# Reordering the booked steps of a Mamba layer's side work around its scans

## The chip, the cores and the metric

The kernel runs on one core of a Trainium2 chip. The metric is the device time of one execution in microseconds (us). A core has five engines that run side by side, each taking its own instructions in program order: TensorE (PE, matrix products into PSUM), VectorE (DVE), ScalarE (ACT, functions and copies), GpSimd (POOL) and SyncE (SP, here the queue that starts most of the DMAs). They wait for each other by semaphores.

## What is computed

The reference is a stack of four pre-normalised residual layers on `x` of shape (2, 128, 56, 56): agent attention, a 3x3 convolution, a mixture of patch experts, and a pair of Mamba scans over image rows. Only the last is touched here. For one way (forward, "f"; "b" runs the row backwards) it is:

```
xi, z = split(x @ in_w.T)
xc = silu(conv_b + sum_k pad(xi)[k : k + L] * conv_w[:, k])
dt, B, C = split(xc @ xproj_w.T, [8, 24])
dt = softplus(dt @ dt_w.T + dt_b)
h[l] = exp(dt[l] * A) * h[l-1] + (dt[l] * xc[l]) * B[l]      # 16 states a channel
y = (sum_s h[l, s] * C[l, s] + xc * D) * silu(z)
out = y @ out_w.T
```

The two ways' results are joined by `fuse_w`, normalised over the channels (mean and variance, scale `ln_w`, shift `ln_b`) and added to `x`.

## The kernel before

`mamba_pair` (from L1532) cuts the work into 14 blocks of 448 positions (8 rows of 56). Each block has two `Half` objects, f and b, and each half has 16 units: 8 pairs of states times two halves of the 256 channels. A unit is one step of the main loop, so a block is a period of `STEPS` = 32 steps: 0 to 15 for f, 16 to 31 for b.

Step n issues, in this order:

- ACT: `decay(n+1)`, two exponentials (L1822) into a `dA` tile in PSUM. There are two such tiles, so it waits until scan n-1 has read its own.
- The fetches due at this step: ACT operations that empty a PSUM bank which PE filled in an earlier step.
- In even steps, unless POOL makes this pair's product: `read_out`, an ACT copy of the pair's C row into the PSUM tile `c_ps` (L1840). In even steps also `send_c`, the DMAs of a later pair's C rows (SP, L1751).
- POOL: `push(n+3)`, the product `dBu` (L1833), four buffers.
- DVE: `scan(n)` (L1852). In odd steps the product of the pair's states with C follows: on DVE from `c_ps` (L1861), or on POOL (L1858) for the pairs in `POOLED`, which are 0, 3, 6 of f and 0, 3 of b. These are steps 0-1, 6-7, 12-13, 16-17 and 22-23.
- DVE: `close`, the gating of y (L1878), when a half's products are all collected. PE: `collect` of the unit three steps back (L1872).
- `run(n)`: the stages booked for this step by hand.

The order of the last item is what the change edits. `book(step, stage, tag, late)` puts a stage in a list; `run` calls it at its step, and if the stage returns a function, that function is the fetch of step + 1 + late. The tag names the PSUM bank that the stage's product takes: "mm" or "c", one bank each, and "c" is also `c_ps`'s bank. A stage that takes a bank waits, on PE, until its last reader is done.

While period p scans block p, the booked stages prepare block p+1, end the preparation of block p's b half and finish block p-1. For a half they are `conv(0)`, `conv(1)` (PE L1703, fetched on ACT L1712 into `xc`), `silu` (L1883 to L1886: a table load, silu of this half's `xc`, silu of the same way's gates `zs` of the block before, and a table load back), `low` (PE L1732, fetched on ACT L1735 into `low`), `send_low` (SP: L1740, L1745), `step(m)` (PE L1757; its fetch is four ACT operations L1767 to L1771), `error(m)` (DVE L1777), `log(m)` (ACT L1782, reads the bank of `step`), `softplus(m)` (PE L1787, fetched by ACT L1788), `weigh` (POOL L1795, L1799), `send_steps` (SP L1810) and `gate(m)` (PE L1720, fetched by ACT L1727). `sp_e` and `sp_u` have one buffer each; `weigh` writes its product over `sp_u`, and the DMAs of `send_steps` read it from there. The finishing of a block is `fuse` (PE L1624, fetched by ACT L1635), `measure` (DVE L1641), `root` (ACT L1648), `newton` (DVE L1657), `normalize` (four ACT operations, L1665), `turn_back` (PE L1676, fetched by ACT L1680) and `onto` (POOL L1686, output DMA L1688).

Of the kernel before, what the change touches and what calls it, by code (L numbers as in the profile page):

```python
# [1531 lines left out]
def mamba_pair(net, out, wts, combine):  # L1532
# [19 lines left out]
    with ExitStack() as ctx:  # L1552
# [327 lines left out]
        def silu(inputs, gates):  # L1880

            if inputs:
                nc.scalar.activation(inputs.xc, inputs.xc, AF.Silu)  # L1883
            if gates:
                nc.scalar.activation(gates.zs, gates.zs, AF.Silu)
            nc.scalar.preload_act_table_set(EXP_LN)  # L1886

        blocks = [Block(b, k) for b in range(NB) for k in range(NBLK)]
# [3 lines left out]
        def book(step, *stages, tag="mm", late=0):  # L1892

            agenda.setdefault(step, []).extend((stage, tag, late) for stage in stages)

        for n, blk in enumerate(blocks):

            f, b = blk.ways
            at = STEPS * (n - 1)
            if n == 0:  # L1900

                book(at + 1, blk.norm)
                book(at + 3, lambda f=f: f.conv(0))
                book(at + 4, lambda f=f: f.conv(1), tag="c")
                book(at + 6, lambda f=f: silu(f, None))
                book(at + 7, f.low)
                book(at + 9, lambda f=f: f.step(0))
                book(at + 9, lambda f=f: f.step(1), tag="c", late=1)
                book(at + 9, f.send_low)
                for m in range(2):  # L1910
                    book(at + 10 + m, lambda f=f, m=m: f.error(m))
                    book(at + 10 + m, lambda f=f, m=m: f.log(m))
                    book(at + 11 + m, lambda f=f, m=m: f.softplus(m), tag=("mm", "c")[m])
                    book(at + 12 + m, lambda f=f, m=m: f.weigh(m))
                    book(at + 12 + m, lambda f=f, m=m: f.send_steps(m))
                for i, (h, m) in enumerate(((f, 0), (f, 1), (b, 0), (b, 1))):
                    book((1, 4, 5, 13)[i], lambda h=h, m=m: h.gate(m))
                book(at + 17, lambda b=b: b.conv(0))
                book(at + 17, lambda b=b: b.conv(1), tag="c")
                book(at + 19, lambda b=b: silu(b, None))  # L1920
                for m in range(2):
                    book(2 + 3 * m, lambda b=b, m=m: b.step(m))
                    book(3 + 3 * m, lambda b=b, m=m: b.error(m))
                    book(4 + 3 * m, lambda b=b, m=m: b.log(m))
                    book(7 + m, lambda b=b, m=m: b.softplus(m))
                book(0, b.low)
                book(2, b.send_low)
                book(11, b.weigh, b.send_steps)
            else:
                before = blocks[n - 1]  # L1930
                book(at + 6, blk.norm)
                book(at + 7, lambda f=f: f.conv(0))
                book(at + 8, lambda f=f: f.conv(1), late=1)
                book(at + 10, lambda f=f, g=before.ways[0]: silu(f, g))
                book(at + 12, lambda b=b: b.conv(0))
                book(at + 12, lambda b=b: b.conv(1), tag="c", late=1)
                book(at + 15, f.low, tag="c")
                book(at + 17, f.send_low)
                book(at + 17, lambda f=f: f.step(0))
                book(at + 18, lambda b=b, g=before.ways[1]: silu(b, g))  # L1940
                book(at + 19, lambda f=f: f.error(0))
                book(at + 19, lambda f=f: f.log(0))
                book(at + 20, lambda f=f: f.step(1))
                book(at + 21, lambda f=f: f.error(1))
                book(at + 22, lambda f=f: f.log(1))
                book(at + 22, lambda f=f: f.softplus(0), tag="c")
                book(at + 23, b.low)
                book(at + 24, lambda f=f: f.softplus(1))
                book(at + 25, f.weigh)
                book(at + 26, lambda f=f: f.gate(0))  # L1950
                book(at + 27, lambda b=b: b.step(0))
                book(at + 27, f.send_steps)
                book(at + 28, lambda b=b: b.error(0))
                book(at + 28, lambda b=b: b.log(0))
                book(at + 29, lambda b=b: b.step(1))
                book(at + 31, lambda b=b: b.error(1))
                book(at + 31, lambda b=b: b.log(1))
                book(at + 32, lambda b=b: b.softplus(0), tag="c")
                book(at + 33, lambda f=f: f.gate(1), late=1)
                book(at + 33, lambda b=b: b.softplus(1), tag="c")  # L1960
                book(at + 33, b.send_low)
                book(at + 35, lambda b=b: b.gate(0))
                book(at + 38, b.weigh)
                book(at + 43, b.send_steps)
                book(at + 46, lambda b=b: b.gate(1), late=1)

            at = STEPS * (n + 1)
            book(at + 4, lambda blk=blk: blk.fuse(0))
            book(at + 4, lambda blk=blk: blk.fuse(1), late=1)
            book(at + 6, blk.measure)  # L1970
            book(at + 7, blk.root, tag="c", late=1)
            book(at + 7, blk.newton)
            book(at + 15, blk.normalize)
            book(at + 16, blk.turn_back)
            book(at + 31, blk.onto)
        for h, step in zip(blocks[-1].ways, (10, 18)):
            book(STEPS * (len(blocks) - 1) + step, lambda h=h: silu(None, h))

        units = [(h, u) for blk in blocks for h in blk.ways for u in range(UNITS)]
# [71 lines left out]
def layers(tc, a, out, wide, attention):  # L2051
    with ExitStack() as ctx:
        net = Net(ctx, tc, a)
        keep = ctx.enter_context(tc.tile_pool(name="keep2", bufs=1, side="right"))
        with tc.tile_pool(name="l1_keep", bufs=1) as taps:
# [5 lines left out]
            with tc.tile_pool(name="l2_w", bufs=2) as wpool:  # L2061
# [44 lines left out]
                with tc.tile_pool(name="l2_work", bufs=2, reuse_waits="tile") as work, tc.tile_pool(  # L2106
                    name="l2_ps", bufs=2, space=PSUM
                ) as ps:
                    experts.run(wpool, work, ps)
        mamba_pair(net, out, wts, experts.combine)  # L2110


# [34 lines left out]
```

## Time and profile before

| What | us |
| --- | --- |
| Median of three runs | 3112.28 |
| The three runs | 3108.09, 3112.28, 3123.26 |
| The profiled execution | 3107.69 |
| Its span | 3105.9 |
| Scan of the first unit starts at | 1731.7 |
| Busy over the span: PE, DVE, ACT, POOL | 2688.7, 2225.7, 1825.4, 1491.6 |
| L1833, POOL, 448 times | 2130 ns each |
| L1852, DVE, 448 times | 2007 ns each |
| L1861, DVE, 154 times | 2021 ns each |
| L1858, POOL, 70 times | 3989 ns each |
| L1822, ACT, 896 times | 636 ns each |

The Mamba layer is the part from 1731.7 us on, somewhat under half of the span. In what follows, a line of the timeline gives the start in us, the length in us, engine, line, operation, what it writes and reads with shapes, how many instructions were merged into it, and in brackets how long the engine had been idle before it and what released it. DVE and ACT instructions that follow each other overlap by about a tenth of a microsecond, so starts are better guides than ends.

### The profile page before, as it was taken

The page shows a single profiled execution, that of the slowest core. Times are in us where ns is not written, and L with a number is a line of the kernel's source. Part 1 is how long each engine was busy: PE and PEld are TensorE (multiplying, and loading weights), DVE is VectorE, ACT ScalarE, POOL GpSimd, SP SyncE. Part 2 cuts the span into 40 slices and gives each one's busy share as a digit, 9 for nine tenths or more (in the row PEclk, how much of TensorE's full clock was granted, in tenths as well). Part 3 has the DMA queues.
Part 4 walks back from the last instruction along what each step waited for, and adds up shares of the span by engine and source line. Part 5 has one row for each costly group of instructions (what it writes and reads, how often), then busy time and mean ns, then how long its engine had stood idle before and what let it go on. Part 6 is the DMA issues. An engine that isn't in the chain of part 4 may idle for free. (4 is left out here: it accounts for less than half of the span.)

```text
span 3105.9 us, 34183 instructions
## 1 busy us (share of the span) xinstructions
PE 2688.7 (87%) x12348; PEld 1055.9 (34%) x12348; DVE 2225.7 (72%) x2033; ACT 1825.4 (59%) x2788; POOL 1491.6 (48%) x801
## 2 busy tenths in 40 slices
PE   7999999999998899999996877888778887778774
PEld 3333333332334444444443322323223333223221
DVE  5879999999887111111112699999999999999996
ACT  5778788887641011111111678777787877777774
POOL 3000100100521000000003799999999999999995
PEclk9999999999998899999997888988888888889886
DMA  1000000000011878787773654564555545545550
GB/s 54 1 1 1 1 1 1 1 1 1 1 38 42 324 280 320 285 318 293 308 299 105 141 115 111 111 142 111 113 126 112 128 112 126 126 109 115 129 125 23
DMA packets 157914, 368.98 MB, mean 119 GB/s; under 512 B 25156, under 2 KB 114980, under 8 KB 154132
## 3 DMA queue, kind: packets, MB, share of 16 engines
q1 hardware_dynamic: 135744, 339.30, 38.0%
q0 software_dynamic: 5520, 15.62, 1.6%
q10 hardware_dynamic: 16452, 11.61, 1.2%
q8 instruction: 101, 1.65, 0.2%
q14 instruction: 97, 0.79, 0.1%
HBM read 297.89 MB, written 17.20 MB: 101 GB/s over the span
## 5 line engine op out<-in xcount | busy, mean ns | idle before, releaser
L1833 POOL TENSOR_TENSOR dBu<-dtu,Bs 128x896 f32<-128x896 f32 x448 | 937.3, 2130 | 61.5 <-DVE h L1852 51.6
L1852 DVE TENSOR_TENSOR_SCAN h<-dA,dBu 128x896 f32<-128x896 f32 x448 | 880.0, 2007 | 64.6 <-ACT dA L1822 47.7
L620 ACT ACTIVATE ex<-sc 128x896 f32<-128x896 f32 (+1 forms) x700 | 602.6, 917 | 124.4 <-PE sc L617 113.2
L1872 PE MATMUL y<-h,both 128*64 128x448 f32 x1792 | 484.1, 639 | 66.4 <-POOL h L1858 55.4
L627 DVE TENSOR_TENSOR ex_sum<-ex_sum,ex 128x1792 f32<-128x1792 f32 (+1 forms) x238 | 492.6, 2070 | 35.1 <-ACT ex L620 21.1
L617 PE MATMUL sc<-q,k 32*128 32x448 f32 (+1 forms) x2800 | 403.4, 587 | 3.6 <-ACT ex L620 2.9
L1341 PE MATMUL h_ps<-w,xs_c 128*128 128x512 f32 x896 | 393.1, 597 | 10.3 <-issue 10.3
L635 PE MATMUL av<-ex,va 128*32 128x448 f32 (+1 forms) x2800 | 334.3, 552 | 0.1
L1861 DVE TENSOR_TENSOR h<-h,c_ps 128x1792 f32<-128x1792 f32 x154 | 311.3, 2021 | 25.5 <-ACT c_ps L1840 10.6
L1822 ACT ACTIVATE dA<-dt,f_A 128x448 f32<-128x448 f32 x448 | 283.8, 636 | 72.9 <-DVE h L1852 48.2
L582 POOL TENSOR_TENSOR a_e<-a_e,a_inv 112x784 f32<-112x784 f32 x14 | 41.6, 2974 | 582.8 <-ACT ex L620 394.5
L1822 ACT ACTIVATE dA<-dt,b_A 128x448 f32<-128x448 f32 x448 | 283.6, 635 | 58.7 <-DVE h L1852 46.7
L1345 DVE TENSOR_TENSOR he<-h_ps,sg 128x512 f32<-128x512 f32 x56 | 38.5, 691 | 381.5 <-PE h_ps L1341 343.8
L1289 POOL DMA_INDIRECT xr<-xd,whom x28 | 28.2, 1006 | 534.7 <-PE xr_ps L1331 489.7
L1858 POOL TENSOR_TENSOR h<-h,Cs 128x1792 f32<-128x1792 f32 x70 | 279.3, 3989 | 1.2 <-issue 1.2
L1872 PEld LDWEIGHTS y<-h,both 128*64 128x64 f32 x1792 | 125.6, 153 | 354.5 <-issue 221.0
L1341 PEld LDWEIGHTS h_ps<-w,xs_c 128*128 128x128 f32 x896 | 168.8, 191 | 218.5 <-issue 202.7
L617 PEld LDWEIGHTS sc<-q,k 32*128 32x128 f32 (+1 forms) x2800 | 137.7, 181 | 230.0 <-issue 132.3
L1362 PE MATMUL o_ps<-w,ht 128*128 128x512 f32 x448 | 197.2, 592 | 0.4 <-ACT ht L1357 0.4
L1344 ACT ACTIVATE sg<-h_ps 128x512 f32<-128x512 f32 x56 | 33.4, 597 | 255.8 <-PE h_ps L1341 255.8
L1364 ACT ACTIVATE ot<-o_ps,share 128x512 f32<-128x512 f32 x28 | 19.3, 688 | 278.9 <-PE o_ps L1362 278.9
L625 DVE TENSOR_TENSOR ex_sum<-ex 128x1792 f32<-128x1792 f32 x56 | 114.4, 2043 | 54.5 <-ACT ex L620 54.5
(333 smaller groups left out, 3023.1 us busy)
## 6 DMA issues: line engine op xcount, KB each, us to landing
w<-in_L_conv_w_dram SPq DMA_DIRECT2D x28, 4096.0 KB, 19.1
w<-in_L_conv_w_dram SPq DMA_DIRECT2D x28, 2048.0 KB, 10.1
Bs<-far SPq DMA_DIRECT2D x56, 896.0 KB, 9.1
Cs<-far SPq DMA_DIRECT2D x448, 112.0 KB, 5.0
dtu<-sp_u SPq DMA_DIRECT2D x108, 224.0 KB, 3.9
dt<-dt SPq DMA_DIRECT2D x108, 224.0 KB, 5.2
os<-ot ACTq DMA_DIRECT2D x28, 256.0 KB, 7.6
xd<-xt SPq DMA_DIRECT2D x14, 224.0 KB, 2.8
```

Source lines behind the costliest of these rows:

```text
L617: nc.tensor.matmul(sc[:size, j, :BLK], self.m.k[rows, at : at + size], self.q[rows, :], start=True, stop=True)
L620: nc.scalar.activation(ex[:size, 2 * g : 2 * g + 2, :], sc[:size, :, :BLK], AF.Exp, scale=scale)
L627: nc.vector.tensor_add(self.total[g][:size], self.total[g][:size], ex[:size])
L635: nc.tensor.matmul(self.av[rows, :BLK], self.m.va[:size, i, rows], self.ex[i][:size, h, :], start=i == 0, stop=i == STEPS - 1,)
L1341: nc.tensor.matmul(h_ps, xc[:, q, :], w1[:, q, f0 : f0 + 512], start=q == 0, stop=q == 3)
L1362: nc.tensor.matmul(o_ps, ht[:, i, :], w2[:, i, :], start=i == 0, stop=i == nj - 1)
L1822: nc.scalar.activation(self.dA[u][:, r * BLK : (r + 1) * BLK], self.dt2[:, m, r, :], AF.Exp, scale=self.w.A[:, j, 2 * m + r : 2 * m + r + 1],)
L1833: nc.gpsimd.tensor_tensor(self.dBu[u], self.dtu2[:, m], self.B[:, j, :].unsqueeze(1).to_broadcast(shape), ALU.mult)
L1852: nc.vector.tensor_tensor_scan(hf, af, bf, 0.0, ALU.mult, ALU.add)
L1858: nc.gpsimd.tensor_tensor(h4, h4, c, ALU.mult)
L1861: nc.vector.tensor_tensor(h4, h4, c, ALU.mult)
L1872: nc.tensor.matmul(self.y[r * H : (r + 1) * H, m, :BLK], both, self.hc[j][:, m, r, :], start=False, stop=j == PAIRS - 1)
```

## The change

It edits only the steps, the bank tags and the `late` marks at which stages are booked. For the preparation of blocks 1 to 13:

- `conv(1)` of f is fetched in step 9 instead of 10.
- `low` of f moves from step 15 (bank "c") to 13 (bank "mm"); its `send_low` from 17 to 15.
- `silu` of b, with the gates of the block before, moves from step 18 to 16.
- `step(0)` of f moves from 17 to 18, and its fetch from 18 to 20. `error(0)` and `log(0)` move from 19 to 21, `step(1)` from 20 to 21 (fetch 22), `error(1)` from 21 to 23, `log(1)` from 22 to 24.
- `low` of b stays in step 23 and takes bank "c" instead of "mm".
- `log(0)` of b moves from step 28 to 29.

For the finishing of every block, `normalize` moves from step 15 to 12 and `turn_back` from 16 to 14. In the last period, the silu of b's gates moves from step 18 to 16.

```diff
-                book(at + 8, lambda f=f: f.conv(1), late=1)
+                book(at + 8, lambda f=f: f.conv(1))
                 book(at + 10, lambda f=f, g=before.ways[0]: silu(f, g))
                 book(at + 12, lambda b=b: b.conv(0))
                 book(at + 12, lambda b=b: b.conv(1), tag="c", late=1)
-                book(at + 15, f.low, tag="c")
-                book(at + 17, f.send_low)
-                book(at + 17, lambda f=f: f.step(0))
-                book(at + 18, lambda b=b, g=before.ways[1]: silu(b, g))
-                book(at + 19, lambda f=f: f.error(0))
-                book(at + 19, lambda f=f: f.log(0))
-                book(at + 20, lambda f=f: f.step(1))
-                book(at + 21, lambda f=f: f.error(1))
-                book(at + 22, lambda f=f: f.log(1))
+                book(at + 13, f.low)
+                book(at + 15, f.send_low)
+                book(at + 16, lambda b=b, g=before.ways[1]: silu(b, g))
+                book(at + 18, lambda f=f: f.step(0), late=1)
+                book(at + 21, lambda f=f: f.error(0))
+                book(at + 21, lambda f=f: f.log(0))
+                book(at + 21, lambda f=f: f.step(1))
                 book(at + 22, lambda f=f: f.softplus(0), tag="c")
-                book(at + 23, b.low)
+                book(at + 23, lambda f=f: f.error(1))
+                book(at + 23, b.low, tag="c")
+                book(at + 24, lambda f=f: f.log(1))
                 book(at + 24, lambda f=f: f.softplus(1))
...
-                book(at + 28, lambda b=b: b.log(0))
+                book(at + 29, lambda b=b: b.log(0))
...
-            book(at + 15, blk.normalize)
-            book(at + 16, blk.turn_back)
+            book(at + 12, blk.normalize)
+            book(at + 14, blk.turn_back)
             book(at + 31, blk.onto)
-        for h, step in zip(blocks[-1].ways, (10, 18)):
+        for h, step in zip(blocks[-1].ways, (10, 16)):
```

## Prediction

> **What bounds the kernel now.** I read the page's busy times, the busy times by stretch, then the timelines of VectorE (DVE), GpSimd (POOL), ScalarE (ACT) and TensorE (PE) over one block of the last layer, and the list of waits. A block is a period of 32 steps, counted 0 to 31 below: 0 to 15 scan the f way, 16 to 31 the b way. I call the two exponentials of L1822 that feed scan n "decay n". ACT issues decay n+1 first in step n; having two dA buffers it must first see scan n-1 end.
>
> The stretches (columns: window, its length, then busy time of PE, weight loads, DVE, ACT, POOL, then clock and DMA):
>
> ```profile
> 2688.90:2784.70 95.80, 77.23 (x254) 28.53 (x252) 90.02 (x63) 74.45 (x127) 91.68 (x43) 0.87 0.54 119
> 2784.70:2880.20 95.50, 76.64 (x254) 27.89 (x252) 90.13 (x63) 74.81 (x128) 91.83 (x44) 0.89 0.55 120
> ```
>
> Scan 0 of consecutive periods starts at 1841.87 and, twelve periods on, at 2988.62: 95.56 us each. POOL works 91.8 of them and DVE 90.1, so neither is full. Who waits for whom decides, and the DVE timeline of the period shows it:
>
> ```profile
> 2791.10 3.94 DVE L1852 TENSOR_TENSOR_SCAN h<-dA,dBu 128x896 f32<-128x896 f32 x2 [0.48 <-ACT dA L1822]
> ...
> 2832.47 7.76 DVE L1852 TENSOR_TENSOR_SCAN h<-dA,dBu 128x896 f32<-128x896 f32 x4 [0.41 <-ACT dA L1822]
> ...
> 2846.88 3.94 DVE L1852 TENSOR_TENSOR_SCAN h<-dA,dBu 128x896 f32<-128x896 f32 x2 [0.67 <-issue]
> 2851.25 2.02 DVE L1861 TENSOR_TENSOR h<-h,c_ps 128x1792 f32<-128x1792 f32 x1 [0.43 <-ACT c_ps L1840]
> ...
> 2857.04 3.94 DVE L1852 TENSOR_TENSOR_SCAN h<-dA,dBu 128x896 f32<-128x896 f32 x2 [2.24 <-ACT dA L1822]
> ```
>
> These are scans 30, 12, 18, the C product after scan 19, and scan 20. They are all of DVE's marked idle time, 4.23 us a period, and ACT is behind each: the 0.67 called "issue" ends 0.09 us after decay 18 (2845.49 + 1.30). POOL is never what DVE waits for here; it waits for DVE, in these lines:
>
> ```profile
> 2799.71 2.12 POOL L1833 TENSOR_TENSOR dBu<-dtu,Bs 128x896 f32<-128x896 f32 x1 [0.97 <-DVE h L1852]
> ...
> 2865.64 2.12 POOL L1833 TENSOR_TENSOR dBu<-dtu,Bs 128x896 f32<-128x896 f32 x1 [2.24 <-DVE h L1852]
> ```
>
> So the bound is a chain of DVE and ACT, with POOL 3.6 us behind it. ACT is busy only 74.8 us; it is late locally. The biggest bubble is made here (ACT, steps 18 and 19):
>
> ```profile
> 2848.57 0.62 ACT L1767 ACTIVATE sp_e<-dt_ps,c_L_conv_f_dt_b 128x448 f32<-128x448 f32 x1
> ...
> 2851.23 1.28 ACT L1883 ACT_TABLE_LOAD   x1
> 2852.52 0.95 ACT L1883 ACTIVATE xc<-xc 128x896 f32<-128x896 f32 x1
> 2853.38 0.93 ACT L1885 ACTIVATE zs<-zs 128x896 f32<-128x896 f32 x1
> 2854.33 1.28 ACT L1886 ACT_TABLE_LOAD   x1
> 2855.63 1.31 ACT L1822 ACTIVATE dA<-dt,b_A 128x448 f32<-128x448 f32 x2
> ```
>
> Four softplus operations (2.12 from start to next), a c_ps copy and a whole silu (4.40) stand between decay 19 and decay 20.
>
> [...] I price silu at the trace's 4.40. [...] "mm" and "c" are single and PE must wait for ACT to empty them; the trace shows PE waiting 3.70 us for L1782 before a dt_ps product. [...] The trace has four y products taking 1.76 us after 2.81 us of idling, against 0.97 in a busy stretch.
>
> **The change part by part.** No operation is added or removed; all is position. From starts in the timelines: a decay holds ACT 1.24, and its scan can start 1.40 after it starts; scans follow at 1.94, a DVE C product takes 1.94 to 2.0, error 0.53, the close (yv) 1.0, copies on ACT 0.45 to 0.55. I replay one period in these durations, on the old time axis.
>
> *conv(1) of f fetched in step 9 instead of 10.* PE is the late one here: it runs without a gap from 2808.6 and ends this conv at 2825.5, whatever the label. Before, decay 11 (2823.99) ran under that wait. Now ACT waits from 2823.7 to 2825.54, does the fetch, then decay 11, c_ps, silu from 2827.9 (was 2826.67). Decay 12 moves to 2832.3, scan 12 from 2832.47 to 2833.7: **+1.24**.
>
> *normalize in step 12* (1.54) sits behind decay 13; decay 14 starts at 2836.3, scan 14 at 2837.72, 0.14 later than it could: **+0.14**. It used to sit in step 15.
>
> *f.low in step 13 on "mm", turn_back in 14, send_low in 15.* Low no longer stands behind the POOL product of steps 12 and 13, which ends the 0.67 (**-0.67**). But a ping-pong over the one "mm" bank forms: low needs conv(0) of b copied out (2838.1), z needs low copied out, gate(1) of b needs z copied out. Low takes 1.8 on a warm PE; I take 2.0 (ends 2840.2), 3.3 at half rate is the other end. ACT then has low 2840.25, c_ps 2840.7, decay 16 at 2841.2, z 2842.45, decay 17 2843.1, gate 2844.35. send_low's three DMAs move two steps up SP's queue, ahead of one pair's C rows; Bs is needed only by push 32, 14 steps on: nothing. If a C row were late, POOL or c_ps would wait, up to the 5 us that its landing takes. On PE, low, z and gate(1) now block the y products of steps 12 to 15 until 2845.4; close of f in step 19 needs them by 2856, so they cost nothing with 10 us of cover. Nothing moves on POOL.
>
> *silu of b in step 16.* It starts at 2844.85 and ends at 2849.25; decay 18 then lets scan 18 start at 2850.65. DVE is ready at 2847.55 (product of 15, scans 16, 17): **+3.1**. Beside a silu lie 2.0 of product and 3.9 of scans, while ACT needs decay 17, gate, silu and decay 18: 1.24 + 0.5 + 4.4 + 1.4 = 7.5 even if punctual, and it enters 1.5 late, since low, z, normalize and two conv copies lie between the silus. What this buys: steps 18 and 19 hold only decays, so **-0.43** and **-2.24**.
>
> *step(0) fetched in 20, error(0) and log(0) in 21, error(1) 23, log(1) 24.* Scan 20 starts at 2857.5. Error(0) is queued on DVE behind scan 21 and its product, at 2863.5 to 2864.1. Log(0) stands on ACT in front of decay 23, so ACT idles 3.3 from 2860.8. Then decay 23 2864.6, four operations of step(1) 2865.85, decay 24 2867.95, scan 24 at 2869.35, when DVE is ready at 2868.55: **+0.8**. PE's step(1) product waits for log(0) too; collects queue behind it, with nobody near.
>
> *b.low on "c" in 23.* It waits for softplus(0) to be copied (2869.7), ends 2871.5; c_ps 2872.0, log(1) 2872.5, so softplus(1) is 2.5 later on PE and copied at 2875.6. Decay 27 comes at 2876.1, scan 27 at 2877.5: **+0.3**, between 0 and 0.9. weigh on POOL, due at 2876.1 after push 28, just gets its input.
>
> *log(0) of b in step 29.* Before, it stood in front of decay 30, waiting 3.36 for the DMA that reads sp_u. Now decay 30 goes first: **-0.48**.
>
> Sum of a period: 1.24 + 0.14 + 3.1 + 0.8 + 0.3 - 0.67 - 0.43 - 2.24 - 0.48 = **+1.76 us**. POOL has room for it (it waits more). Thirteen periods prepare a next block and pay it; in the last, POOL runs from 2992.8 to 3071 with no gap, so nothing is added there. 13 x 1.76 = 23 us on the profiled execution's 3107.69 (span 3105.9 and 1.8 around it): 3130.6. That execution lies at the low end of 3108 to 3123, median 3112.28; on the median it would be 3135. I take 3131. Ends: a fast low and no wait at scan 27 give +1.25 a period (3124); half-rate low (+1.3) and 0.9 at scan 27 give +3.6 (3154).
>
> **The rivals.** *Faster*: ACT arrives punctually at step 16. If decay 16 starts when scan 14 ends and the wait of step 9 costs nothing (PE's conv done by 2823.7), scan 18 waits 1.55, and a period is 1.55 + 0.14 + 0.8 - 3.82 = -1.3: 3091. For it: a POOL-only period would be 92.2, so DVE could take the gain. Against: PE's gapless run up to 2825.5, and ACT's work from silu to decay 18, 20.8 us plus 1.4 to the scan, against 17.7 of DVE. It decides once ACT is less than 0.4 late at step 16. *A wash*: the stalls at scans 18 and 24 come, but DVE's lateness lets ACT and PE regroup elsewhere, or period 0 (110 us, with waits of its own) absorbs its share; +0.7 a period, 3121. *Worse*: PE half-rate in the ping-pong and in softplus, weigh late, push 32 later: 3153. That the change doesn't do what it says: steps 16 and 17 are a pair whose product POOL makes; only step 15's lies beside silu.
>
> **How the numbers follow.** Forecast 0.58, wash 0.20, faster 0.12, worse 0.10. About 0.5% (16 us) is what a measurement of this kernel can tell from no change; of the forecast 0.08 lies inside it, of the faster case 0.02, of the wash 0.01 outside. Slower 0.61, same 0.29, faster 0.10. The range leaves out the faster case and a few of the worse: 3112 to 3151.
>
> **What would show it.** Right: periods of about 97.3; DVE waits of some 1.6 before scan 12, 3 before scan 18, 0.8 before scan 24, none before scans 20 and 30; ACT idling 1.8 before xc in step 9 and 3 before log(0) in step 21. Wrong: a period under 95, scan 18 waiting under 1.5, or POOL without idle time.

## The result and the profile after

| | Before | After |
| --- | --- | --- |
| Median of five runs, us | 3115.54 | 3153.54 |
| Lowest, highest | 3108.09, 3123.26 | 3152.69, 3158.31 |
| The profiled execution | 3107.69 | 3153.54 |
| Its span | 3105.9 | 3151.2 |
| Its mean PE clock | 0.925 | 0.918 |

After over before is 1.0125, with a 95% interval of 1.0103 to 1.0147. The forecast was 3131, in a range of 3112 to 3151: slower as predicted, by about twice as much, and just outside the range.

The two spans differ by 45.3 us. Twelve steady periods take 98.67 each instead of 95.56 (scan 0 starts at 1848.61 and, twelve periods on, at 3032.6): 37.3 us. Period 0 takes 114.81 instead of 110.18, 4.6 more. The Mamba layer starts 2.1 later, and its last part is 1.3 longer.

The stretches, for the period that starts at 1946.49 (I call it period 2) and one that starts at 2834.66 (columns: window, its length, busy time of PE, weight loads, DVE, ACT, POOL, then clock and DMA):

```profile
1946.49:2043.80 97.31, 73.86 (x253) 27.89 (x252) 90.25 (x63) 74.70 (x126) 92.31 (x43) 0.91 0.52 117
2834.66:2933.64 98.98, 77.65 (x253) 28.93 (x252) 90.48 (x63) 74.68 (x126) 92.38 (x43) 0.86 0.51 115
```

Both are periods of the same program. The first takes 97.31, which is what was forecast; the second 1.67 more, with 3.8 more busy time of PE for the same 253 products at a lower clock. From the fourth steady period on, all nine take 98.98 to 99.00. The DVE timeline of the long period:

```profile
2843.73 2.02 DVE L1861 TENSOR_TENSOR h<-h,c_ps 128x1792 f32<-128x1792 f32 x1 [1.25 <-ACT c_ps L1840]
...
2854.97 0.87 DVE L1641 BATCH_NORM_STATS2 ln_st<-ln_y 112x6 f32<-112x128 f32 x4 [0.31 <-ACT ln_y L1635]
...
2872.93 7.92 DVE L1852 TENSOR_TENSOR_SCAN h<-dA,dBu 128x896 f32<-128x896 f32 x4 [2.02 <-ACT dA L1822]
...
2889.49 3.94 DVE L1852 TENSOR_TENSOR_SCAN h<-dA,dBu 128x896 f32<-128x896 f32 x2 [2.66 <-POOL dBu L1833]
...
2896.47 3.93 DVE L1852 TENSOR_TENSOR_SCAN h<-dA,dBu 128x896 f32<-128x896 f32 x2
...
2908.32 3.94 DVE L1852 TENSOR_TENSOR_SCAN h<-dA,dBu 128x896 f32<-128x896 f32 x2 [0.66 <-ACT dA L1822]
...
2916.57 2.02 DVE L1852 TENSOR_TENSOR_SCAN h<-dA,dBu 128x896 f32<-128x896 f32 x1 [0.25 <-ACT dA L1822]
...
2927.14 3.93 DVE L1852 TENSOR_TENSOR_SCAN h<-dA,dBu 128x896 f32<-128x896 f32 x2
```

In order: the C product after scan 3, measure, then scans 12, 18, 20, 24, 27 and 30. The last six are as the prediction placed them: waits at 12, 18, 24 and 27, none at 20 and 30. The first two were foreseen by no step. The ACT timeline shows what stands before scan 18:

```profile
2883.15 0.52 ACT L1727 COPY zs<-gate_ps 128x448 f32<-128x448 f32 x1
2883.69 1.28 ACT L1883 ACT_TABLE_LOAD   x1
...
2886.79 1.28 ACT L1886 ACT_TABLE_LOAD   x1
2888.09 2.54 ACT L1822 ACTIVATE dA<-dt,b_A 128x448 f32<-128x448 f32 x4
```

The wait of scan 18 is labelled "POOL dBu". That product had ended at 2885.2; decay 18 ends 1.3 after 2888.09, just before the scan. So the label names an event that the scan also waits for, and here it isn't the one that was late.

**Where the unforeseen part comes from.** The PE timeline at softplus(0) of b (L1787), first in period 2, then two periods later, in a long one. In brackets is how long PE had been idle:

```profile
1946.09 1.02 PE L1787 MATMUL sp_ps<-sp_u,ident 128*128 128x448 f32 x2 [2.30 <-DVE h L1861]
1946.95 0.92 PE L1787 MATMUL sp_ps<-sp_e,minus 128*128 128x448 f32 x2
1947.70 0.92 PE L1787 MATMUL sp_ps<-dt,ident 128*128 128x448 f32 x2
...
2141.35 1.02 PE L1787 MATMUL sp_ps<-sp_u,ident 128*128 128x448 f32 x2 [2.13 <-DVE h L1861]
2142.20 1.40 PE L1787 MATMUL sp_ps<-sp_e,minus 128*128 128x448 f32 x2
2143.40 1.70 PE L1787 MATMUL sp_ps<-dt,ident 128*128 128x448 f32 x2
```

From the first start to the last end the same six products take 2.53 in one period, at a mean granted clock of 1.00, and 3.75 in the other, at 0.65. In the long period softplus(1), which follows on PE, is late by that much. So the `dt` copy that fetches it (L1788) comes late, `c_ps` stands behind it on ACT, and the C product after scan 3 waits (the ACT timeline of the long period, then DVE in both):

```profile
2149.68 0.53 ACT L1788 COPY dt<-sp_ps 128x448 f32<-128x448 f32 x1 [2.60 <-PE sp_ps L1787]
```

```profile
1954.41 2.02 DVE L1861 TENSOR_TENSOR h<-h,c_ps 128x1792 f32<-128x1792 f32 x1
...
2150.81 2.02 DVE L1861 TENSOR_TENSOR h<-h,c_ps 128x1792 f32<-128x1792 f32 x1 [1.25 <-ACT c_ps L1840]
```

Why the rate differs can be read from the clock. In the traces of before and after the granted clock is always either 1.00 or 0.50, and it changes only on a fixed grid: from its first change to its last (775.76 to 3089.99 in before, 777.17 to 3135.78 in after) every change lies a whole number of 3.4133 us behind the first, within 0.005. One such step of the grid is a window in the expectations below. Here are two stretches of the grid in each period, around the idle spell (columns: window, its length, PE busy, clock, DMA):

```profile
1944.53:1947.94 3.41, 1.85 (x5) 1.00 0.32 109
1947.94:1951.36 3.42, 3.42 (x11) 1.00 0.29 82
...
2139.09:2142.50 3.41, 1.27 (x5) 1.00 0.21 76
2142.50:2145.91 3.41, 3.41 (x8) 0.50 0.22 76
```

In period 2 a boundary of the grid, at 1944.53, divides the idle spell. The stretch behind it still has PE busy for 1.85, and the next one stays at 1.00. In the long period the whole spell lies in one stretch, PE is busy for 1.27 of it, and the next one is granted 0.50.

In the kernel before, PE was idle for only 0.82 ahead of this product, since its y products ran until just before; its products run at full rate (granted clock 1.00 from 2797.22 to 2799.75):

```profile
2791.65 4.75 PE L1872 MATMUL y<-h,both 128*64 128x448 f32 x12
2797.22 1.02 PE L1787 MATMUL sp_ps<-sp_u,ident 128*128 128x448 f32 x2 [0.82 <-DVE h L1861]
2798.07 0.92 PE L1787 MATMUL sp_ps<-sp_e,minus 128*128 128x448 f32 x2
2798.83 0.92 PE L1787 MATMUL sp_ps<-dt,ident 128*128 128x448 f32 x2
```

In after these y products end 1.3 earlier against scan 0. Read from the timelines, not tested by a run: log(0) of b, which had waited 3.36 for a DMA in before, no longer waits (it starts 9.7 ahead of scan 0 instead of 8.3), and on PE the product of step(1) and these y products follow it. A wait that went away on ACT opened the idle spell on PE.

A second such place lies 10 us later in the long period. The first line is from before, the other two from after:

```profile
2806.90 1.04 PE L1720 MATMUL gate_ps<-pad,b_gate_t 128*128 128x448 f32 x2 [1.99 <-ACT zs L1727]
...
2845.45 1.71 PE L1720 MATMUL gate_ps<-pad,b_gate_t 128*128 128x448 f32 x2 [1.99 <-ACT zs L1727]
2846.95 2.73 PE L1868 MATMUL y<-xc,f_skip 128*128 128x448 f32 x4
```

The idle spell ahead of the gate is 1.99 in both kernels, and in period 2 of after as well. Only its place on the grid differs. The granted clock over the two gate products is 0.56 in this period, and 1.00 in the line of before and in period 2, where they take 1.04 and 1.03. The four L1868 products behind it take 2.73 at a clock of 0.61, and in before 1.77 at 1.00. The slow products delay fuse, and with it measure (0.31 above), and the wait of scan 12 is 2.02, where it is 1.58 in period 2. The conv that it waits for comes later in PE's queue.

### The profile page after: what moved, and what is told of

Read it like the earlier page. It is cut to its first block, busy times and chain, and to the rows that moved or that the text cites. A ratio compares the mean times of both kernels' runs of the same rounds, so it can differ in the third digit from the quotient of the medians.

```text
span 3151.2 us, 34171 instructions
## 1 busy us (share of the span) xinstructions
PE 2695.2 (86%) x12348; PEld 1065.7 (34%) x12348; DVE 2231.0 (71%) x2033; ACT 1826.8 (58%) x2788; POOL 1500.8 (48%) x801
## 5 line engine op out<-in xcount | busy, mean ns | idle before, releaser
L1872 PE MATMUL y<-h,both 128*64 128x448 f32 x1792 | 472.7, 630 | 25.4 <-DVE h L1861 15.4
```

What stands on the lines that cost most here:

```text
L1872: nc.tensor.matmul(self.y[r * H : (r + 1) * H, m, :BLK], both, self.hc[j][:, m, r, :], start=False, stop=j == PAIRS - 1)
```

## The experiments

The theory: the order costs about what the sum said, and the rest is PE running at half rate after idle spells (**clock**). The rivals: the waits that the sum foresaw are larger than reckoned and push each other on (**order**), or a step that I credited (log(0) of b, conv(1)) costs elsewhere. The means to tell them apart is to keep PE busy: products with a zero weight, accumulated into y, so that they add nothing to any result.

```diff
+    def zeros(self, u, count):
+        j, m = self.unit(u)
+        for i in range(count):
+            nc.tensor.matmul(self.y[:H, m, :BLK], nought, self.hc[j][:, m, i % 2, :], start=False, stop=False)
...
+        nought = work.tile([P, H], F32, name="nought", tag="nought", bufs=1)
+        nc.vector.memset(nought, 0.0)
```

**a_warm: zero products ahead of softplus(0) of b, in after.** Four in step 29 and eight in step 31.

```diff
+                book(at + 29, lambda h=before.ways[1]: h.zeros(10, 4))
+                book(at + 31, lambda h=before.ways[1]: h.zeros(12, 8))
```

> The changed kernel plus products of a zero weight tile, added into y (they add nothing): four ahead of step(1) of b in step 29 and eight in step 31, where TensorE otherwise idles about 2.8 and 2.1 us. Theory clock: those idle spells let TensorE's clock fall, its softplus(0) products in step 0 take 4.1 us instead of 2.7, and from that come the waits of 1.25 us before the C product of step 3, 0.3 before measure and 0.4 of the 2.0 before scan 12; with the spells filled these go, a period falls from 98.98 to about 97.3, and the time from 3153 to about 3132. Rival order: the waits come from the booked order alone; then nothing is won, and the added products make it the same or a few us slower, 3153 to 3160.

Measured: 3152.91, ratio to before 1.0124 (1.0107 to 1.0141). A miss of the instrument: eight were too many. They were still running when softplus(0) could start, which began 1.74 after the end of the C product of step 31 instead of 0.06 after it. The wait at the C product after scan 3 stayed at 1.29. It decides nothing.

**a_warm5: the same with five in step 31.**

> As the earlier run with zero products, but sized so that they end in time: four ahead of step(1) of b in step 29 and five in step 31 (0.775 us each in that run's trace, where eight overshot by 1.7 us). Theory clock: softplus(0) now starts on a warm TensorE as soon as the C product of step 31 is done; the wait of 1.25 us before the C product of step 3 goes, and a period falls from 98.98 to between 97.3 and 97.8: 3153 - 13 x 1.3 = 3136. If the clock drops at another spell instead, the period stays 98.98. Rival order: 3153, with the wait before the C product of step 3 kept at 1.25.

Measured: 3155.39, ratio 1.0134 (1.0111 to 1.0156). The PE timeline shows the place mended and another spoiled:

```profile
2538.04 1.02 PE L1787 MATMUL sp_ps<-sp_u,ident 128*128 128x448 f32 x2 [0.49 <-DVE h L1861]
...
2649.16 3.36 PE L1868 MATMUL y<-xc,f_skip 128*128 128x448 f32 x4 [0.67 <-DVE yv L1883]
```

The wait after scan 3 is gone in 11 of 12 periods, those in which softplus(0) starts on time and at a clock of 1.00. So its cause is shown: it is the clock at softplus(0). But the time isn't won. The half rate now falls elsewhere (3.36 above for the four products that take 1.77 in before at a clock of 1.00), and measure waits 0.8, the C product after scan 15 0.7 to 0.8, scan 18 up to 3.46. Here mending one spell only moved the slow products to the next.

**a_conv10: conv(1) of f fetched in step 10 again, in after.**

```diff
-                book(at + 8, lambda f=f: f.conv(1))
+                book(at + 8, lambda f=f: f.conv(1), late=1)
```

> The changed kernel with conv(1) of f fetched in step 10 again. Theory order: ACT does decay 11 under the wait for TensorE again, scan 12 waits 1.24 us less in each of 13 periods: 3153 - 16 = 3137. Rival clock lock: the period sits on 29 windows of TensorE's clock (98.98 us); then the 1.24 us comes back as another wait, and the time stays within 6 us of 3153 or drops by more than 20 once the lock breaks.

Measured: 3143.74, ratio 1.0092 (1.0073 to 1.011). The DVE timeline:

```profile
2839.18 2.02 DVE L1861 TENSOR_TENSOR h<-h,c_ps 128x1792 f32<-128x1792 f32 x1 [1.88 <-ACT c_ps L1840]
...
2867.21 3.94 DVE L1852 TENSOR_TENSOR_SCAN h<-dA,dBu 128x896 f32<-128x896 f32 x2 [1.04 <-ACT dA L1822]
```

Scan 12 waits 0.98 less, but 0.63 of it comes back after scan 3, and 0.43 as a new wait of scan 3. The twelve steady periods take 98.70 on the mean, where after has 98.67: one takes 95.58, one 99.34, most of the others 98.98. So nothing is won in the steady periods, for which the edit was priced. Of the 7.1 by which the profiled span is shorter than that of after, 5.1 come from period 0 (109.72 instead of 114.81), the rest from an earlier start and a shorter end. The local price is right and the period doesn't follow it.

**a_log28: log(0) of b in step 28 again, in after.**

```diff
-                book(at + 29, lambda b=b: b.log(0))
+                book(at + 28, lambda b=b: b.log(0))
```

> The changed kernel with log(0) of b in step 28 again. Theory clock: the later log(0) keeps TensorE blocked longer in step 29, its idle spell before softplus(0) shrinks, the clock stays up: the C product of step 3 no longer waits 1.25 us, scan 30 waits up to 0.5 again: 3153 - 13 x 0.75 to 1.5 = 3133 to 3143. Rival order: log(0) in 28 only puts the wait for the DMA back ahead of decay 30: 3153 + 6 = 3159.

Measured: 3156.73, ratio 1.0134 (1.0117 to 1.0151). No wait changes: the C product after scan 3 keeps its 1.25, and scan 30 waits for nothing even with log(0) in its old step. Both theories of this edit fall, though 3159 lay near. The wait of scan 30 isn't gone because of this edit. In after, weigh of f starts 5.3 us ahead of scan 28, in before 3.5 ahead, so the DMA that log(0) waits for is done in time.

**a_silu18: the silu of b in step 18, after step(0), in after.**

```diff
-                book(at + 16, lambda b=b, g=before.ways[1]: silu(b, g))
                 book(at + 18, lambda f=f: f.step(0), late=1)
+                book(at + 18, lambda b=b, g=before.ways[1]: silu(b, g))
...
-        for h, step in zip(blocks[-1].ways, (10, 16)):
+        for h, step in zip(blocks[-1].ways, (10, 18)):
```

> The changed kernel with silu of b in step 18 again (and that of the last gates), while step(0) stays fetched in step 20. The wait of 2.66 us before scan 18 goes; silu now lies beside scans 18 and 19, the C product of 19 and the close, 6.9 us, while ACT needs decay 19, c_ps, silu and decay 20, about 7.5: a wait of 0.6 before scan 20. Theory order: 3153 - 13 x 2.0 = 3127. Rival: ACT is late into step 18 from the stages before it, so that the wait only moves to scan 20 at 2.2 or more, and the time stays within 6 us of 3153.

Measured: 3145.95, ratio 1.011 (1.0089 to 1.013). The wait of scan 18 is gone and scan 20 waits 0.67, so the 2.66 belonged to the silu, whatever its label. But 8 us are won instead of 26: scan 25 now waits 1.34, the C product after scan 15 0.81, and measure 0.86, in most periods.

**b_silu20: the opposite, from before. The silu of b two steps later instead of two earlier.**

```diff
-                book(at + 18, lambda b=b, g=before.ways[1]: silu(b, g))
-                book(at + 19, lambda f=f: f.log(0))
+                book(at + 20, lambda b=b, g=before.ways[1]: silu(b, g))
+                book(at + 20, lambda f=f: f.log(0))
                 book(at + 20, lambda f=f: f.step(1))
-                book(at + 21, lambda f=f: f.error(1))
+                book(at + 22, lambda f=f: f.error(1))
                 book(at + 22, lambda f=f: f.log(1))
...
-        for h, step in zip(blocks[-1].ways, (10, 18)):
+        for h, step in zip(blocks[-1].ways, (10, 20)):
```

> The kernel before with silu of b in step 20 instead of 18, log(0) behind it, error(1) in 22. ACT's 4.4 us then lie beside the C product of 19, the close, error(0) and scans 20 and 21. Theory order: the wait of 2.24 before scan 20 goes, one of 0.35 before scan 23 comes: 95.56 - 1.9 = 93.7 a period, 3112 - 13 x 1.9 = 3088. Rival clock lock: TensorE's clock drops at other spells and pulls the period back to 28 windows, 95.57: 3112, within 5 us of the kernel before.

Measured: 3106.14, ratio 0.9981 (0.9974 to 0.9988). The DVE timeline:

```profile
2567.99 3.93 DVE L1852 TENSOR_TENSOR_SCAN h<-dA,dBu 128x896 f32<-128x896 f32 x2
...
2577.02 5.85 DVE L1852 TENSOR_TENSOR_SCAN h<-dA,dBu 128x896 f32<-128x896 f32 x3 [0.52 <-ACT dA L1822]
...
2624.13 0.88 DVE L1641 BATCH_NORM_STATS2 ln_st<-ln_y 112x6 f32<-112x128 f32 x4 [0.85 <-ACT ln_y L1635]
```

Scan 20's 2.24 is gone and scan 23 waits 0.52 in its place, 1.7 a period to the good. Yet the mean period falls only from 95.56 to 95.33: in half of the periods measure waits some 0.85 as in a_silu18, and in five of twelve scan 18 waits 1.3 instead of 0.4 to 0.7. In both directions an order that is better by DVE's waits hardly gains in time; the runs with zero products below show how much of that is the clock.

**a_delay and b_delay: a delay of DVE in step 9, in after and in before.**

```diff
+        def idle_away(w):
+            for _ in range(2):
+                nc.vector.scalar_tensor_tensor(w.gate, w.gate, 1.0, w.gate, ALU.mult, ALU.max)
+
...
+                book(at + 9, lambda f=f: idle_away(f.w))
```

> The changed kernel plus two VectorE operations on a constant (they leave it as it is), about 0.7 us in step 9 of each period. Theory order: every steady period grows by 0.7, to 99.7. Rival clock lock: the steady period stays at 98.98, since the wait before scan 12 shrinks by what is added in front of it or the clock drops less deep.

> The kernel before plus the same two VectorE operations, about 0.7 us in step 9 of each period. Ahead of scan 12 they take up to 0.4 to 1.0 of its wait. Theory order: 95.56 + 0.3 = 95.9 a period. Rival clock lock: the mean of the periods stays 95.57, 28 windows.

Measured, one run each: 3195.32 and 3157.74, with mean periods of 102.35 and 99.70. The instrument was mis-sized. The pair took 4.56 in the line below (b_delay, DVE timeline) instead of 0.7, and scan 12's wait vanished into it. What the two runs were to tell apart, they don't.

```profile
2269.71 4.56 DVE L1890 SCALAR_TENSOR_TENSOR f_gate_t<-f_gate_t 128x256 f32<-128x256 f32 x2
```

**a_warmall, b_warm, b20_warm: zero products in all the idle spells.** In after 22 (two in step 13, two in 14, six in 17, two in 27, three in 29, five in 31 and two in the next period's step 1); in before, and in b_silu20, 17 (three in step 14, three in 17, two in 27, four in 29, three in 31 and two in step 1).

```diff
+                book(at + 17, lambda h=before.ways[0]: h.zeros(13, 6))
+                book(at + 27, lambda h=before.ways[1]: h.zeros(6, 2))
...
+                book(at + 33, lambda h=before.ways[1]: h.zeros(13, 2))
```

> The changed kernel with zero products added into y at every idle spell of TensorE over about 1.5 us (steps 1, 13, 14, 17, 27, 29 and 31 of a period, 22 in all, 0.4 to 0.8 us each). Theory clock: no spell is long enough for the clock to drop, all products run at full rate, only the waits of the prediction's sum are left: periods of about 97.3, 3153 - 12 x 1.6 = 3134. Rival: the extra waits stand in the booked order, or the zero products delay TensorE as much as the clock did: periods of 98.5 and more, 3148 to 3160.

> The kernel before with zero products at its idle spells (steps 1, 14, 17, 27, 29, 31). Theory clock: the wait before scan 12 stays at 0.41 in every period and low of f ends sooner, 95.2 a period or a little less: 3108, up to 10 less. Rival: nothing changes or the added products delay: 3112 to 3120.

> The kernel before with silu of b in step 20 and the same zero products. Theory clock: the 1.9 us a period that the move should have given, and of which the trace without zero products showed 0.2, comes out: about 93.6 a period, 3112 - 12 x 1.9 = 3089. Rival: the gain was lost to the order of the instructions, not to the clock: 3106, as without the zero products.

Measured, in this order: 3135.03 (3131.79 to 3140.32), ratio 1.0055 (1.0034 to 1.0077); 3100.97 (3093.65 to 3105.57), ratio 0.995 (0.9931 to 0.9969); 3089.02 (3084.59 to 3091.78), ratio 0.9908 (0.9884 to 0.9933). The stretches of one period of each:

```profile
2529.42:2626.54 97.12, 86.61 (x297) 32.94 (x296) 90.35 (x63) 74.55 (x126) 92.37 (x43) 0.96 0.53 118
```

```profile
2329.05:2423.42 94.37, 84.92 (x286) 31.50 (x286) 89.79 (x63) 74.64 (x128) 92.28 (x43) 0.96 0.56 122
```

```profile
2032.99:2126.34 93.35, 84.78 (x287) 31.81 (x286) 89.79 (x64) 74.53 (x126) 92.21 (x43) 0.96 0.55 122
```

PE is busy for 8 to 9 us more a period (86.61 against 77.65, 84.92 against 76.64), and all three run faster than the same order without the zero products: the clock is 0.96. If it is only ever 1.00 or 0.50 here too, as in the traces of before and after, some 8% of the period is still at half rate (an estimate from the 0.96), against 22% in before (from its 0.89) and 28% in after (from its 0.86). The zero products aren't free: in three of b_warm's twelve periods and in two of a_warmall's they and the y products behind them ran on when softplus(0) could have started, and the C product after scan 3 waited 1.1 to 1.2 and 0.7. The PE and DVE timelines of a_warmall show the places at full rate, and the waits that are left:

```profile
2821.49 1.02 PE L1787 MATMUL sp_ps<-sp_u,ident 128*128 128x448 f32 x2
2822.35 0.92 PE L1787 MATMUL sp_ps<-sp_e,minus 128*128 128x448 f32 x2
...
2831.03 1.03 PE L1720 MATMUL gate_ps<-pad,b_gate_t 128*128 128x448 f32 x2 [0.49 <-ACT zs L1727]
2832.38 1.77 PE L1868 MATMUL y<-xc,f_skip 128*128 128x448 f32 x4 [0.32 <-DVE yv L1883]
```

```profile
2565.44 7.93 DVE L1852 TENSOR_TENSOR_SCAN h<-dA,dBu 128x896 f32<-128x896 f32 x4 [1.58 <-ACT dA L1822]
...
2776.22 3.94 DVE L1852 TENSOR_TENSOR_SCAN h<-dA,dBu 128x896 f32<-128x896 f32 x2 [2.65 <-issue]
...
2795.06 3.94 DVE L1852 TENSOR_TENSOR_SCAN h<-dA,dBu 128x896 f32<-128x896 f32 x2 [0.66 <-ACT dA L1822]
```

This gives the split. With PE nearly always at full rate on both sides, the order costs 3135.03 - 3100.97 = 34 us. The low clock costs after 3153.54 - 3135.03 = 18.5 us, and before 3114 (the runs of before beside these) - 3101 = 13 us. So of the 39 us between the two kernels the order makes about 34, 11 more than my sum, and the clock about 5. The spread of the five and seven runs leaves the 34 open by some 5 us to each side (an estimate), so 23 is excluded, but the clock's 5 can't be told from nothing. The theory that the order makes 23 and the clock the rest falls. What the clock took in before it takes in after at other places, which is why single waits in the profile of after do show it. b20_warm beats both kernels. That it came to the 3089 that was expected is luck in part: its mean period is 94.20, not 93.6, and of the 12 us that its profiled span is shorter than b_warm's 4.7 lie in period 0. In the twelve steady periods the later silu wins 0.6 each (94.20 against 94.78), not the 1.9 that its waits promised, so the clock explains a part of that shortfall and not all.

**aw_conv10, aw_silu18, aw_log28: the three undoings again, in a_warmall,** where the clock blurs them less. The edits are those of a_conv10, a_silu18 (with four zero products in step 17) and a_log28.

> The changed kernel with zero products at all idle spells and conv(1) of f fetched in step 10 again. Theory: with TensorE warm the single terms of the prediction hold; the wait before scan 12 falls from 1.58 by 1.0 to 1.24 and nothing takes its place: periods of 96.0, 3135 - 13 x 1.1 = 3121. Rival: what was given back without zero products was given back by the order, not the clock: 3131 to 3137.

> The changed kernel with zero products and silu of b in step 18 again (zero products in step 17: four instead of six). Theory: the wait of 2.66 before scan 18 goes, 0.67 before scan 20 comes, nothing else: periods of 95.1, 3135 - 13 x 2.0 = 3109. Rival: later waits take it, as in the run without zero products where 0.8 a period was left: 3125.

> The changed kernel with zero products and log(0) of b in step 28 again. Theory: the prediction's term of 0.48 before scan 30 comes back, or less, since weigh now comes earlier against the scans: periods of 97.1 to 97.6, 3135 to 3141. Rival: log(0) in step 29 is itself what costs: 3125 or less.

Measured: 3125.99, ratio 1.004 (1.0029 to 1.0052); 3115.17, ratio 0.9997 (0.9979 to 1.0014); 3134.16, ratio 1.0068 (1.0048 to 1.0089). In the first, scan 12 waits 0.41 instead of 1.58, scan 18 3.31 instead of 2.65, and the period is 96.60 instead of 97.12. So the conv's 1.17 is real, but half of it only made scan 18 wait longer; of the 10.5 between the two profiled spans 4.6 come from the twelve steady periods and 3.8 from period 0. The second takes back 20 us, between what the theory and the rival said: scan 18 waits no more, 0.67 comes at scan 20 and, in most periods, 0.6 after scan 3. The third changes nothing.

## Why the prediction was half right

The ledger of a steady period, as differences of after against before (the profile of before alternates between 0.41 and 1.03 at scan 12, and between some 0.68 and 0.42 at scan 18; the means over the twelve steady periods are 0.67 and 0.56). The measured column takes a long period of after against these means. The last column is a_warmall against b_warm:

| Term of the sum, us a period | Forecast | Measured | At full rate |
| --- | --- | --- | --- |
| Scan 12 (conv(1)) | +1.24 | 2.02 - 0.67 = +1.35 | +1.17 |
| Scan 14 (normalize) | +0.14 | +0.16 | +0.16 |
| Scan 18 (silu, less the credit for low) | 3.1 - 0.67 | 2.66 - 0.56 = +2.10 | +2.65 |
| Scan 24 (step(1)) | +0.8 | +0.66 | +0.66 |
| Scan 27 (low of b) | +0.3 | +0.25 | +0.25 |
| C product after 19, scans 20 and 30 | -3.15 | -3.19 | -3.1 |
| C product after scan 3 | none | +1.25 | none |
| Measure, scan 11 | none | 0.32 + 0.24 | none |

The measured column sums to 3.14. A long period is 98.98 - 95.56 = 3.42 longer, and the stretches show DVE itself some 0.4 longer busy (90.48 against 90.02 and 90.13), so nothing of size is missing from the column. Over all twelve steady periods the growth is 3.11, since the first three are shorter.

**What held.** The direction, every wait that the sum foresaw, within 0.45 a period, and the signposts on ACT: it idles 1.84 before `xc` in step 9 (forecast 1.8) and 3.32 before log(0) in step 21 (forecast 3). No wait of DVE in the ledger goes back to POOL or SP.

**The step that failed: in "The change part by part", half rate was priced for one stage.** The prediction took it for low alone (1.8 to 3.3), and every other product at full rate. The rest it named only in the "worse" rival, "PE half-rate in the ping-pong and in softplus", 3153 with a chance of 0.10, and that is the time that came, by softplus and the gate and not by the ping-pong. The upper end of the sum, 3154, names the same time, but for other reasons: low at half rate and 0.9 at scan 27. Low took 1.70 in every steady period of after, at full rate, and scan 27 waited 0.25. The replay of DVE, ACT and POOL should have gone on to PE: how long is PE idle ahead of each short product that somebody waits for, and where on the clock's grid? Ahead of softplus(0) of b the spell went from 0.82 to 2.1. Ahead of the gate it stayed at 1.99, and only its place on the grid changed. These two places, which the sum put at nothing, give the last two rows, +1.81. The prediction's own line of half rate, 1.76 instead of 0.97, stood behind a spell of 2.81. Here spells of 1.9 to 2.4 were enough, depending on their place on the grid (in after softplus(0) of b at a granted clock of 0.59 to 0.65, the gate at 0.56).

**The credit of -0.67 was real in before, and for the wrong reason.** The prediction had low standing behind the POOL product. In b_warm low stands where it stood, and the wait is gone all the same: it was low running partly at half rate (its four products take 2.2 to 2.6 in the steady periods of before, at a granted clock of 0.65 to 0.74, and 1.67 in b_warm, from nearly the same start). So the gain was a clock cost that left one place, as others came. At full rate there is nothing to credit. Without the credit the sum is 2.43 a period, 32 us in thirteen, close to the 34 of the full-rate pair: the prices of the order were nearly right, and the sum went wrong by the clock, which it took out of one place and put in at none.

**What the full-rate pair leaves open.** The period of a_warmall is 2.75 longer than b_warm's (97.12 and 94.37). The column above gives 1.79, and the error of step 28, which waits 0.27 in a_warmall, makes it 2.06. Most of the other 0.7 is DVE's own busy time, 90.35 against 89.79 in the stretches: consecutive operations overlap by about 0.1 (two scans in a row take 3.94 where one takes 2.02), and one that has waited doesn't. Over all twelve periods the difference is 2.47 (97.25 and 94.78).

**The sum was carried to period 0 as it stood.** It grew by 4.6, not 1.76; its C product after scan 9 waits 7.79 instead of 3.56. This is the clock again, and not the order: in after the f conv that it waits behind takes 5.21 there, at a granted clock of 0.62, and softplus(0) of b ahead of it 4.84, at 0.50, against 3.31 and 2.53 in before, both at 1.00. The same wait is 7.8 in b_warm and b_silu20, which have the old order there, and 3.56 in a_conv10 and aw_log28, which have the new one.

**Against the rivals.** *Faster* fails: ACT enters silu late, as argued (2883.69 to 2888.09, then decay 18). *A wash* fails: nothing regrouped in the new order's favour, and undoing its two costly parts gave time back. That log(0) of b in step 29 takes away scan 30's wait was right in the number and wrong in the cause (a_log28, aw_log28).

**Still open in part: why so many periods have the same length.** They are 98.98 in after, in a_log28 and mostly in a_conv10, although their waits differ; before averages 95.56, and a_delay 102.35. These lengths lie near whole numbers of the 3.4133 us that separate the boundaries of the clock's grid in the traces of before and after. Estimates from it: 28 windows are 95.57, 29 are 98.99, 30 are 102.40. The traces also show that the periods keep step with the grid. In after, from the fourth steady period on, every scan 0 starts 2.67 behind a boundary, and the same products fall into the half-rate windows each time (in all nine the clock is 0.65 over softplus(0) of b and 0.56 over the gate). In before two periods (95.3 and 95.8) make 56 windows, and in a_warm5 two (98.3 and 99.8) make 58. With zero products throughout, a_warmall's 97.12 and b_warm's 94.4 keep no step. So a loop whose waits depend on where its idle spells fall can settle on whole windows, and then win nothing from a local repair: a_conv10 and a_warm5 each removed a wait and kept a mean of 98.7 and 98.9. It isn't a rule: a_silu18 (94.8 to 100.2, mean 98.20) and b_delay (99.2 to 100.7, mean 99.70) don't sit on a whole number. That the step with the grid is what ate the repairs is argued from these periods; no run moved the grid against the kernel.

## What to carry to other kernels

In a loop bound by who waits for whom, cost a reordering on two ledgers: the waits of the chain, and the idle spells that it opens ahead of short TensorE products that others wait for. A spell of 2 us nearly doubled such a product here (0.92 to 1.70; at another place on the clock's grid it left it at 0.92), though TensorE, busy 78% of the period, wasn't the bound. Before judging single edits of an order, fill the spells with zero products, so that the clock stays up (0.96 here, against 0.89 and 0.86 a period); the edits here then moved the time nearer to what their waits say (20 us of silu instead of 8), and the filling by itself was worth 0.5%.

## What the runs showed of the hardware that was not expected

- Extra TensorE work made both kernels faster: 8 to 9 us more busy time a period, and 13 us less in all for before (b_warm), 18 for after (a_warmall).
- The same products, after the same idle spell, run at either rate: 0.92 after 2.30 of idling, 1.70 after 2.13, in two periods of one execution. In the long period the spell fell into one 3.41 us stretch of the clock's grid, which left PE 1.27 busy in it; in the other a boundary divided it. In the steady periods of after, every full-rate stretch with PE under 47% busy was followed by half rate, and none with over 68%; in between both occur.
- The two-input DVE operation of the delay runs took 0.42 whenever POOL was idle, and 4.08 to 5.14 in b_delay when it met two or three POOL products in a row. It ended 0.28 after the last of them; in b_delay it never ended between POOL products that followed each other closely (in a_delay it did once). L1777, with one input in PSUM, stayed at 0.60 to 0.63. Why the one takes longer beside POOL and the other doesn't, no run shows.
